# Sorting the first layer's batches by expert too, so that pairs of them share one weight product: a two-layer mixture-of-experts kernel on one NeuronCore

## The chip, the core and the metric

The kernel runs on one NeuronCore of a Trainium2 chip. TensorE (PE) multiplies matrices into PSUM, VectorE (DVE), ScalarE (ACT) and GpSimd (POOL) do the rest, each works through its own instructions in order, and SyncE (SP) issues most DMAs. The metric is the device time of one execution in microseconds. All data are float32.

## The reference, cut to what matters

```
x: (16, 256, 256)   cond: (16, 8)          # 16 batches, 256 rows, width 256; 8 experts
# layer 0: each batch by the expert of its largest cond
e = argmax(cond, -1)
up, gate = x @ W_up[e].T + b_up[e], x @ W_gate[e].T + b_gate[e]        # width 512
x = x + (silu(up) * gate) @ W_down[e].T + b_down[e]
# layer 1: each batch by its two largest experts, weighted, plus one shared expert
w, sel = top_k(softmax(cond), 2); w = w / w.sum()
mlp(x, g, u, d) = (gelu(x @ g) * (x @ u)) @ d                          # width 1024
out = x + sum_k w_k * mlp(x, skill[sel_k]) + mlp(x, shared)
```

## The kernel before

Batches lie transposed (128 partitions, two halves of the width, 256 rows). The product of one 128x128 weight block and one batch's 256 columns is one matmul; the trace records each as two halves. A batch alone needs 24 matmuls in layer 0 and 48 in layer 1.

**Pairs.** Two batches that use the same weights form a 2x2 block product: weight blocks A11 to A22 against B11, B21 (first batch) and B12, B22 (second). `STEPS` writes this product with seven block products in place of eight (Strassen's idea in Winograd's form): sums of weight blocks (`sums_a`, on POOL, into tiles `s` and `ds`), sums of activations (`sums_b`, on DVE), and results combined from three PSUM banks X, Q and Y (two buffers each; the down product uses A, B and Y). A pair's work on one quarter of the hidden width is a "quarter": seven steps of two matmuls, copies by ACT, combinations by DVE.

**Layer 0** (class `First`) takes the batches in their own order, each alone: `up(0)`, `up(1)`, and the `down()` of the batch before. Its expert comes from `first_largest` on the logits `lg`. The result goes to `x1d` (a DRAM tensor that layer 1 reads) and to `out_dram`, in rows fixed when the kernel is built (L348, L349, on POOL's queue).

**Layer 1** works on units: eight shared pairs of batches (2i, 2i+1), and 32 (batch, expert) entries sorted by expert with pairs first, of which 24 always form 12 pairs (`NP2`) and 8 are left as singles. The sort (`choices`, `order_of_work`) compares all 32 entries with all 32 on DVE, 1024 elements a step, and is dealt out among layer 0's batches. Expert and batch numbers of the sorted units are read into registers at run time (`held`). Two shared pairs come first, then skill pairs, seven singles, and six shared pairs with the eighth single (`lone`) among the first of them. Each unit adds its result to `out_dram` by an accumulating DMA (`add_out`, L442). The last pair reads what `out_dram` holds into `z` and stores the sum itself (L545, SP's queue).

**The order of the work** is written out by hand. `quarters` lists all quarters; `Line.quarter` at the start of each issues the weight load five quarters ahead (`Q_AHEAD`), POOL's sums and the x load three ahead (`S_AHEAD`), and the x sums one ahead. `Line.main` runs a step and advances a clock; `Line.later` puts work (a quarter's seventh step, its activation, a pair's seven down steps) some ticks behind.

Of the kernel before, what the change touches and what calls it, by code (L numbers as in the profile page):

```python
# [7 lines left out]
F32 = mybir.dt.float32  # L8
# [8 lines left out]
P = 128  # L17
KD = D // P
K0 = H0 // P
KP = H1 // P // 2  # L20
NPR = B // 2
NA = 2 * B

NP2 = (NA - E) // 2
N2 = 2 * S
W0 = KD * H0
WH = W0 // 2
OG = W0 + 2 * K0 + KD
F0 = OG + W0
# [28 lines left out]
def kernel(  # L58
# [4 lines left out]
    w0: bass.AP,  # L63
    w0d: bass.AP,
    wq: bass.AP,
    wd: bass.AP,
# [17 lines left out]
    def square(name):  # L84
        return work.tile([P, NA, NA], F32, tag="bt", name=name, bufs=7)

# [4 lines left out]

    def x_load(pr):
        t = work.tile([P, KD, N2], F32, tag="x0", name=f"x_{pr}", bufs=3)
        nc.sync.dma_start(t, x[pr])
        return t

    xs = {0: x_load(0)}
# [13 lines left out]
    num = const.tile([P, NA], F32, name="num")  # L111

# [4 lines left out]
    idx1 = const.tile([P, B], I32, name="idx1")  # L117
# [17 lines left out]
    at0 = const.tile([1, 1], F32, name="at0")  # L135
    idx0 = const.tile([1, 1], I32, name="idx0")
    first_largest(lg0, 0, at0)
    as_index(idx0, at0, E, E - 1)
    at1 = ats[:, :B]
    m1 = first_largest(lg, 1, at1)  # L140
    as_index(idx1, at1, E, E - 1)
    for i in range(NA):
        nc.gpsimd.memset(num[:, i : i + 1], float(i))


    exs_i = const.tile([P, NA], I32, name="exs_i")
    bs_i = const.tile([P, NA], I32, name="bs_i")
    wsort = const.tile([P, NA], F32, name="wsort")
    nwsort = const.tile([P, NA], F32, name="nwsort")

    def choices():

        hot = [const.tile([P, B, E], F32, name=f"hot_{k}") for k in range(2)]
        nc.vector.tensor_tensor(hot[0], em8b, over_experts(at1), ALU.is_equal)
        lg2 = const.tile([P, B, E], F32, name="lg2")
        nc.vector.tensor_scalar(lg2, hot[0], -2.0, 1.0, ALU.mult, ALU.add)
        nc.vector.scalar_tensor_tensor(lg2, lg2, FLT_MAX, lg, ALU.mult, ALU.min)
        at2 = ats[:, B:]
        first_largest(lg2, 2, at2)
        nc.vector.tensor_tensor(hot[1], em8b, over_experts(at2), ALU.is_equal)  # L160
        nc.vector.tensor_scalar(ats, ats, float(-E), -1.0, ALU.max, ALU.min)
        rw = const.tile([P, B, E], F32, name="rw")
        nc.vector.tensor_tensor(rw, lg, over_experts(m1), ALU.subtract)
        nc.scalar.activation(rw, rw, AF.Exp)
        tot = const.tile([P, B], F32, name="tot")
        nc.vector.tensor_reduce(tot, rw, AX.X, ALU.add)
        nc.vector.reciprocal(tot, tot)
        nc.vector.tensor_tensor(rw, rw, over_experts(tot), ALU.mult)
        wts = const.tile([P, 2, B], F32, name="wts")
        for k in range(2):  # L170
            nc.vector.tensor_tensor(hot[k], rw, hot[k], ALU.mult)
            nc.vector.tensor_reduce(wts[:, k, :], hot[k], AX.X, ALU.add)
        den = const.tile([P, B], F32, name="den")
        nc.vector.tensor_tensor(den, wts[:, 0, :], wts[:, 1, :], ALU.add)
        nc.vector.reciprocal(den, den)
        wsc = const.tile([P, 2, B], F32, name="wsc")
        for k in range(2):
            nc.vector.tensor_tensor(wts[:, k, :], wts[:, k, :], den, ALU.mult)
        nc.vector.tensor_scalar(wsc, wts, SCALE, None, ALU.mult)
        nc.vector.scalar_tensor_tensor(wts, wts, 1.0 - SCALE, wsc, ALU.mult, ALU.add)  # L180
        return wts.rearrange("p k b -> p (k b)")

    def rows_of(t):
        return t.unsqueeze(2).to_broadcast([P, NA, NA])

    def cols_of(t):
        return t.unsqueeze(1).to_broadcast([P, NA, NA])

    def small(name):
        return const.tile([P, NA], F32, name=name)  # L190

    def order_of_work(wts):

        tt, red = nc.vector.tensor_tensor, nc.vector.tensor_reduce
        ab = square("ab")
        rank, count, base, left, pos, t = map(small, ("rank", "count", "base", "left", "pos", "t"))
        paired = small("paired")  # L200
        tt(ab, rows_of(ats), cols_of(ats), ALU.is_equal)
        yield
        red(count, ab, AX.X, ALU.add)
        yield
        low = square("low")
        tt(low, rows_of(num), cols_of(num), ALU.is_gt)
        yield
        tt(ab, ab, low, ALU.mult)
        yield
        red(rank, ab, AX.X, ALU.add)  # L210
        yield

        ci = const.tile([P, NA], I32, name="ci")
        nc.vector.tensor_copy(ci, count)
        nc.vector.tensor_single_scalar(ci, ci, -2, ALU.bitwise_and)
        nc.vector.tensor_copy(count, ci)
        tt(paired, rank, count, ALU.is_lt)
        yield
        tt(ab, rows_of(ats), cols_of(ats), ALU.is_gt)
        yield  # L220
        tt(ab, ab, cols_of(paired), ALU.mult)
        yield
        red(base, ab, AX.X, ALU.add)
        yield
        tt(base, base, rank, ALU.add)

        nc.vector.tensor_scalar(left, paired, -1.0, 1.0, ALU.mult, ALU.add)
        tt(low, low, cols_of(left), ALU.mult)
        yield
        red(t, low, AX.X, ALU.add)  # L230
        yield
        n_paired = const.tile([P, 1], F32, name="n_paired")
        red(n_paired, paired, AX.X, ALU.add)
        yield
        nc.vector.tensor_scalar(t, t, n_paired, None, ALU.add)
        tt(base, base, t, ALU.subtract)
        tt(base, base, paired, ALU.mult)
        yield
        tt(pos, base, t, ALU.add)
        at = square("at")  # L240
        tt(at, rows_of(num), cols_of(pos), ALU.is_equal)
        yield

        def sorted_(dst, v):
            got = square("got")
            tt(got, at, v, ALU.mult)
            red(dst, got, AX.X, ALU.add)

        sorted_(t, cols_of(ats))
        yield  # L250
        as_index(exs_i, t, E, E - 1)
        nb = num[:, :B].unsqueeze(1).unsqueeze(1).to_broadcast([P, NA, 2, B])
        got = square("got")
        tt(got.rearrange("p s (k b) -> p s k b", k=2), at.rearrange("p s (k b) -> p s k b", k=2), nb, ALU.mult)
        yield
        red(t, got, AX.X, ALU.add)
        yield
        as_index(bs_i, t, 0, B - 1)
        sorted_(wsort, cols_of(wts))
        yield  # L260
        nc.vector.tensor_scalar(nwsort, wsort, -1.0, None, ALU.mult)
# [11 lines left out]
    def l0_load(b):  # L273
        e = held(idx1, b, E - 1) if b else held(idx0, 0, E - 1)
        src = w0[bass.ds(e, 1)].rearrange("e p f -> (e p) f")
        w = wp.tile([P, OG], F32, tag="q", name=f"w0u_{b}", bufs=6), wp.tile(
            [P, W0], F32, tag="s", name=f"w0g_{b}", bufs=5
        )
        if b == 0:
            for lo, hi in ((0, WH), (WH, OG)):  # L280
                nc.sync.dma_start(w[0][:, lo:hi], src[:, lo:hi])
                nc.sync.dma_start(w[1][:, lo : lo + WH], src[:, OG + lo : OG + lo + WH])
        else:
            nc.sync.dma_start(w[0], src[:, :OG])
            nc.sync.dma_start(w[1], src[:, OG:])
        wdn = wp.tile([P, W0], F32, tag="ds" if b % 2 else "d", name=f"w0d_{b}")
        nc.sync.dma_start(wdn, w0d[bass.ds(e, 1)].rearrange("e p f -> (e p) f"))
        return w, wdn

    class First:  # L290


        def __init__(self, b):
            self.b = b
            self.w, self.wdn = l0_load(b)
            self.hid = work.tile([P, K0, S], F32, tag="bt", name=f"hid_{b}", bufs=7)

        def up(self, hh):
            b, w = self.b, self.w
            pr, cols = b // 2, bass.ts(b % 2, S)  # L300
            bu = w[0][:, W0 : W0 + K0]
            bg = w[0][:, W0 + K0 : W0 + 2 * K0]
            pu = bank("X", f"pu_{b}_{hh}").rearrange("p (j s) -> p j s", j=2)
            pg = bank("Q", f"pg_{b}_{hh}").rearrange("p (j s) -> p j s", j=2)
            for dst, wt in ((pu, w[0]), (pg, w[1])):
                wt = wt[:, bass.ts(hh, WH)].rearrange("p (c h) -> p c h", c=KD)
                for j in range(2):
                    for c in range(KD):
                        nc.tensor.matmul(  # L309
# [519 lines left out]
```

## Time and profile before

| | |
|---|---|
| median of 3 runs | 1072.04 us (1071.8 to 1072.36) |
| the profiled execution: time, span | 1072.31 us, 1070.7 us |
| busy: PE, DVE, ACT, POOL | 1065.7, 647.8, 310.9, 449.4 us |
| granted TensorE clock | 1.0 |
| TensorE records | 4906, of them 10 of the warm-up spin (6.99 us) |
| DMA | 152.56 MB, 142 GB/s over the span; 306 to 426 GB/s from 8 to 29 us, where layer 0 loads ahead |

In the profile a line such as `L462 DVE TENSOR_TENSOR c<-u,Q 128x512` names the line of the kernel, the engine, the operation and the tiles; a duration is that of one instruction or of a merged group (`x8`); a bracket tells how long the engine was idle before it and what it waited for. A matmul record lasts 380 ns but a new one starts every 216 ns, so TensorE's pace is read from starts. The span is the time from the first to the last instruction; the execution's own time is 1.6 us longer.

### The profile page before, as it was taken

How to read it: one execution, taken by the hardware profiler on the slowest of the kernel's cores; microseconds unless marked ns; L12 is line 12 of the kernel's file. 1: busy time of each engine (PE TensorE's matmuls, PEld its weight loads, DVE VectorE, ACT ScalarE, POOL GpSimd, SP SyncE). 2: the span in 40 equal slices, each digit the busy share in tenths (PEclk: the TensorE clock that was granted, in tenths of full speed). 3: DMA queues.
4: the chain of work that ended last, by engine and by line, in shares of the span. 5: the costliest groups of instructions: out<-in, count | busy, mean ns of one | idle time of the engine just before them, and what ended most of it. 6: DMA issues, size and time to landing. Idle time of an engine off the chain costs nothing.

```text
span 1070.7 us, 13745 instructions
## 1 busy us (share of the span) xinstructions
PE 1065.7 (100%) x4906; PEld 932.0 (87%) x4906; DVE 647.8 (61%) x985; ACT 310.9 (29%) x507; POOL 449.4 (42%) x514
## 2 busy tenths in 40 slices
PE   9999999999999999999999999999999999999998
PEld 7888888888888888888888888888888888888887
DVE  5842234877778877877777876311112467777774
ACT  2111114333333333333333333111111333333331
POOL 0111145656635754665466542010002745664520
PEclk9999999999999999999999999999999999999999
DMA  8656763633553354345425532556656443454132
GB/s 331 214 194 222 267 232 104 212 106 90 138 138 99 98 138 132 91 113 138 115 90 131 138 96 77 163 138 202 180 168 203 142 152 106 126 138 107 51 80 39
DMA packets 50805, 152.56 MB, mean 142 GB/s; under 512 B 5298, under 2 KB 16178, under 8 KB 47154
## 3 DMA queue, kind: packets, MB, share of 16 engines
q1 hardware_dynamic: 36690, 131.24, 36.3%
q0 software_dynamic: 14048, 20.45, 10.7%
q8 instruction: 39, 0.64, 0.2%
q14 instruction: 28, 0.23, 0.1%
HBM read 130.70 MB, written 20.97 MB: 142 GB/s over the span
## 4 chain that ended last, share of the span: by engine, by line
PE 100%; DVE 0%; issue 0%
PE X L475 19%; PE Y L475 13%; PE Q L475 13%; PE dX L517 10%; PE dQ L517 6%; PE dY L517 6%; PE pg L309 5%; PE pg L590 5%; PE po L608 5%; PE po L337 5%; PE pu L309 5%; PE pu L590 5%; PE spin L105 1%; DVE idle L102 0%; DVE ys L541 0%
## 5 line engine op out<-in xcount | busy, mean ns | idle before, releaser
L458 ACT ACTIVATE u<-X 128x512 f32<-128x512 f32 x240 | 143.2, 597 | 408.1 <-PE X L475 407.8
L442 POOL DMA_DIRECT2D out_dram<-ys x46 | 47.8, 1040 | 380.0 <-ACT ys L618 138.2
L475 PE MATMUL X<-xt,s 128*128 128x256 f32 x640 | 164.8, 380 | 0.1
L475 PE MATMUL Y<-xt,q 128*128 128x256 f32 x640 | 164.3, 379 | 0.0
L475 PE MATMUL Q<-xt,s 128*128 128x256 f32 x640 | 164.2, 379 | 0.0
L501 DVE TENSOR_TENSOR bt<-c 128x1024 f32<-128x1024 f32 x80 | 106.9, 1336 | 83.8 <-ACT c L499 83.8
L475 PEld LDWEIGHTS X<-xt,s 128*128 128x128 f32 x640 | 120.9, 190 | 18.7 <-issue 2.3
L475 PEld LDWEIGHTS Y<-xt,q 128*128 128x128 f32 x640 | 121.5, 190 | 17.0 <-DVE c L462 0.4
L475 PEld LDWEIGHTS Q<-xt,s 128*128 128x128 f32 x640 | 121.6, 190 | 16.5
L462 DVE TENSOR_TENSOR c<-u,Q 128x512 f32<-128x512 f32 x160 | 108.8, 680 | 27.7 <-ACT u L458 25.4
L462 DVE TENSOR_TENSOR c<-u,Y 128x512 f32<-128x512 f32 x160 | 108.5, 678 | 9.3 <-PE Y L475 9.3
L419 POOL TENSOR_TENSOR s<-q 128x256 f32<-128x256 f32 x80 | 68.9, 862 | 81.7 <-PE Q L475 62.0
L600 DVE TENSOR_TENSOR act<-gel,pu 128x512 f32<-128x512 f32 x32 | 22.0, 688 | 124.7 <-PE pu L590 124.7
L499 ACT ACTIVATE c<-c 128x1024 f32<-128x1024 f32 x80 | 84.1, 1052 | 11.3 <-DVE c L462 11.1
L475 PE MATMUL X<-xt,q 128*128 128x256 f32 x320 | 82.1, 379 | 0.0
L517 PE MATMUL dX<-bt,ds 128*128 128x256 f32 x320 | 75.6, 379 | 0.0
L517 PE MATMUL dY<-bt,d 128*128 128x256 f32 x320 | 75.6, 379 | 0.0
L517 PE MATMUL dQ<-bt,ds 128*128 128x256 f32 x320 | 75.6, 379 | 0.0
L421 POOL TENSOR_TENSOR s<-q 128x256 f32<-128x256 f32 x80 | 73.5, 919 | 0.0
L348 POOL DMA_DIRECT2D x1d<-x x16 | 11.1, 696 | 138.3 <-DVE x L345 129.3
L412 DVE TENSOR_TENSOR bt<-bt 128x512 f32<-128x512 f32 x80 | 69.1, 864 | 0.0
L422 POOL TENSOR_TENSOR s<-s,q 128x256 f32<-128x256 f32 x80 | 68.3, 853 | 0.0
(108 smaller groups left out, 1530.9 us busy)
## 6 DMA issues: line engine op xcount, KB each, us to landing
q<-wq_dram SPq DMA_DIRECT2D x112, 512.0 KB, 3.5
d<-wd_dram SPq DMA_DIRECT2D x28, 1024.0 KB, 6.6
xt<-x1d SPq DMA_DIRECT2D x48, 256.0 KB, 4.4
out_dram<-ys POOLq DMA_DIRECT2D x46, 256.0 KB, 6.0
w0d<-w0d_dram SPq DMA_DIRECT2D x16, 512.0 KB, 8.8
w0u<-w_dram SPq DMA_DIRECT2D x15, 517.0 KB, 7.2
w0g<-w_dram SPq DMA_DIRECT2D x15, 512.0 KB, 8.2
x<-x_dram SPq DMA_DIRECT2D x8, 512.0 KB, 3.4
```

The source lines that it names most:

```text
L309: nc.tensor.matmul(dst[:, j, :], lhsT=wt[:, c, bass.ts(j, P)], rhs=xs[pr][:, c, cols], start=(c == 0), stop=(c == KD - 1),)
L412: tt(t[:, 4:6, :], t[:, 0:3:2, :], t[:, 2:4, :], ALU.subtract)
L419: tt(s("S1"), a("A21"), a("A22"), ALU.add)
L421: tt(s("nS3"), a("A21"), a("A11"), ALU.subtract)
L422: tt(s("nS4"), s("S2"), a("A12"), ALU.subtract)
L458: nc.scalar.activation(t, self.banks["X", j], AF.Copy)
L462: nc.vector.tensor_tensor(self.c[j][:, block].rearrange("p m s -> p (m s)"), self.copies[n, j], self.banks[tag, j], op,)
L475: nc.tensor.matmul(self.banks[tag, j][:, bass.ts(m, S)], lhsT=self.q[j][:, m, A_AT[a], :] if a in A_AT else self.s[j][:, m, S_AT[a], :], r ...
L499: nc.scalar.activation(c[:, :, 0, :], c[:, :, 0, :], AF.Gelu_apprx_tanh)
L501: nc.vector.tensor_tensor(t[:, 0:4, :], c[:, :, 0, :], c[:, :, 1, :], ALU.mult)
L517: nc.tensor.matmul(d, lhsT=src[:, j, :], rhs=self.acts[j][:, B_AT[b], :], start=OPENS[k] and j == 0, stop=j == KP - 1, skip_group_check=True,)
L590: nc.tensor.matmul(dst[:, bass.ts(half, S)], lhsT=self.q[j][:, m, 2 * half + c, :], rhs=self.xt[:, c, :], start=(c == 0), stop=(c == KD - 1),)
```

## The change

Layer 0 becomes units like layer 1's. Batch 0 (`First`) is still computed alone and at once. The 15 batches behind it are sorted by expert, with pairs first; whatever the data, four pairs (`NP1`) can be formed, and seven batches stay single.

- `order_of_work(n, at, layer)` is the sort for both layers, rewritten: one key (the entry's expert times n plus its number, plus 4096 if it has no partner) and its rank. For layer 0 it runs on 16x16 comparisons, all at once, at the start (batch 0 gets key 0 and sorts to an unused place); for layer 1 it is dealt out by `next(routing)`: six steps between batch 0's two quarters, five at each of the next two quarters, one at each after that.
- Layer 0's weights are laid out as layer 1's (`wq0`, `wd0`), with the bias columns behind the blocks. A pair of layer 0 is two quarters of seven steps and seven down steps of two matmuls, three ticks apart, begun 18 ticks after its last quarter. `act` adds the biases (`scalar_tensor_tensor`, Silu); `early` adds the residual and the down bias.
- A layer 0 single is cut in pieces (`ups`: both quarters, 16 matmuls; `downs`: 8), one piece after each quarter of a layer 0 pair or of the first shared pairs (`among`). One single's quarters run before the first pair.
- Batch numbers of layer 0 and of the shared pairs (which now pair batches as sorted, `batches_at`) are read at run time, for loads and for the writes of `x1d` and `out_dram`. Three shared pairs (`NF`) stand ahead of the skill pairs.
- Results are sent at the start of the next quarter, behind POOL's sums there (`done`, `send`), but at once for the second last unit. The last pair's stores go to SP's queue for one batch and to ScalarE's for the other.

```diff
-    for b in range(B):
-        firsts.append(First(b))
...
-        if b < B - 2:
-            firsts[b].up(0)
-            firsts[b].up(1)
-            if b:
-                firsts[b - 1].down()
...
+    l0_first = First(next(names), 0, B - 1)
+    l0_pairs = [Pair(next(names), 0, 2 * i) for i in range(NP1)]
+    l0_ones = [Single(next(names), 0, 2 * NP1 + i) for i in range(NS1)]
+    shared = [Pair(next(names), 1, None, (2 * i, 2 * i + 1)) for i in range(NPR)]
...
+    units = [*l0_pairs, *shared[:NF], *pairs, *ones[:-1], *shared[NF:]]
...
+    pieces = [p for u in l0_ones[1:] for p in (u.ups, u.downs)]
+    pieces.insert(0, l0_ones[0].downs)
+    places = [a for u in units[: NP1 + NF] for a in among[u]]
...
+    for j in range(l0_first.kp):
+        l0_first.load_q(j, 2)
+    l0_first.load_d()
+    m1 = first_largest(lg, 1, at1)
...
+    for _ in order_of_work(B, sort1, 0):
+        pass
+    routing = choices()
+    for j in range(2):
+        l0_ones[0].load_q(j)
+    l0_ones[0].load_x()
+    l0_pairs[0].load_q(0)
+    line.at = 0
+    l0_first.up(0)
+    line.ahead(0)
+    for _ in range(6):
+        next(routing)
+    line.at = 1
+    l0_first.up(1)
+    line.ahead(1)
+    l0_first.downs()
+    l0_ones[0].ups()
...
+                if self.layer:
+                    nc.gpsimd.dma_start(row(out), ys[:, :, t, :], accum_op=ALU.add)
+                else:
+                    nc.gpsimd.dma_start(row(x1d), ys[:, :, t, :])
+                    nc.gpsimd.dma_start(row(out), ys[:, :, t, :])
...
+                    queue = (nc.sync, nc.scalar)[t]
+                    store = queue.dma_start(self.out[t][:, c, :], dst)
```

## The prediction

> **What bounds the kernel now.** I read the page first, for which engine is full, then the chain of waits and the timeline of the places that the change touches.
>
> ```profile
> PE 1065.7 (100%) x4906; PEld 932.0 (87%) x4906; DVE 647.8 (61%) x985; ACT 310.9 (29%) x507; POOL 449.4 (42%) x514
> ...
> PE 100%; DVE 0%; issue 0%
> ```
>
> TensorE is never idle between its first matmul and its last, so the time is the number of matmuls times their pace, plus the two ends. The chain of waits in order of time (start and length in us, engine, line, records) gives the pace:
>
> ```profile
> 8.59 1.73 PE pu L309 x8
> ...
> 22.40 3.45 PE po L337 x16
> ...
> 32.76 3.45 PE po L337 x16
> ```
>
> One batch of layer 0 (24 matmuls, which the trace records as 48 halves) repeats every 32.76 - 22.40 = 10.36 us: 0.216 us a half, 0.432 us a matmul, 0.863 us a pair's step of two. A change gains by removing matmuls; it loses wherever another engine makes TensorE wait, which so far none does.
>
> **Matmuls.** Removed: 15 batches x 24 = 360 in layer 0. Added: four pairs x 42 (two quarters of 14, and 14 down) and seven singles x 24 = 336. Layer 1 keeps its own. 24 fewer is exactly one batch's row: **-10.36 us**. The built instruction order of the two kernels has the same difference (2429 matmuls against 2453), so "it does not do what it says" is no rival. Biases, residuals and the copies of the bias columns lie on other engines and cost TensorE nothing while those keep up; the rest of the sum asks where they don't.
>
> **The start.** So far expert numbers for batch 1 were ready at 6.5 us and loads ran ahead. Now nothing behind batch 0 can be loaded before 15 batches are sorted, and VectorE, which sorts, also makes batch 0's activations. From the timeline (start, length, engine, line):
>
> ```profile
> 5.03 0.29 DVE L126 TENSOR_REDUCE m<-lg 128x16 f32<-128x128 f32 x1 [2.06 <-DMA lg<-cond_dram]
> 5.35 0.29 DVE L128 TENSOR_TENSOR cand<-lg,m 128x128 f32<-128x128 f32 x1
> ...
> 22.89 1.22 DVE L201 TENSOR_TENSOR ab<-ats 128x1024 f32<-128x1024 f32 x1
> 24.14 1.22 DVE L203 TENSOR_REDUCE count<-ab 128x32 f32<-128x1024 f32 x1
> ...
> 31.36 0.18 DVE L215 TENSOR_SCALAR ci<-ci 128x32 int32<-128x32 int32 x1
> 31.57 0.18 DVE L216 CAST count<-ci 128x32 f32<-128x32 int32 x1
> ```
>
> Steps of 128 elements follow each other every 0.32 us, small ones every 0.21, those of 1024 every 1.25; 256 elements (16x16) interpolate to 0.45. From 5.03: four steps of the choice 1.3, three more 0.7, ten of 256 4.5, eight small 1.7, the index 0.2: experts at 13.4 us; two more of 256 and an index: batches at 14.5. Two activations of batch 0 (0.44 each, the pitch of L324) end at 15.4, when TensorE, from 8.59, has done batch 0's two quarters (15.5). Then the order puts ten steps of the second choice (the kind of L154 to L166, 2.9 us by their pitch) ahead of the second quarter's activations: those run 18.3 to 19.2. TensorE has used up the first quarter's by 17.2, so it waits and ends batch 0 at about 20.7 instead of 18.95: **+1.7** (0.9 if the logits land 0.8 us sooner, 256 KB less of x ahead of them at the 331 GB/s of that slice; 2.5 if 0.8 later).
>
> *Loads behind it.* The earlier kernel took 0.7 us from the index (2.97) to the first weight load (3.69), so the second batch's quarters are issued at 14.1 and 14.7, its x at 15.3. A 512 KB load lands in 3.5 us in layer 1, a 256 KB one in 4.4, but w0g took 8.2 in layer 0 with loads piled up. SP has nothing to issue from about 6.5 to 14, so the queue is empty and I take layer 1's: x at 19.7, before TensorE is free, cost nothing. With 8.2 it lands at 23.5: +2.8.
>
> *The clock.* In the spin, a weight load takes 0.34 us until 6.03 and 0.19 after 6.7: the array starts slow and speeds up after about 5 us of work. [...] The sum goes by the row: no gap there, no fall, nothing added.
>
> *The squares.* The sort for layer 1 (32x32) is dealt out one step to a quarter, but three go between the second batch's two activations. VectorE: first activations to 25.2 (matmuls end 24.15), x sums 1.6, six small steps 1.25, three squares 3.7, second activations 0.9: 32.7. TensorE needs the Y bank that they read at 20.7 + 16 x 0.432 + 5 x 0.863 = 31.9. So +0.9 alone, and more with contention:
>
> ```profile
> 307.32 0.43 DVE L413 TENSOR_TENSOR bt<-bt 128x256 f32<-128x256 f32 x1
> ...
> 315.73 1.93 DVE L413 TENSOR_TENSOR bt<-bt 128x256 f32<-128x256 f32 x1
> 316.15 1.21 POOL L419 TENSOR_TENSOR s<-q 128x256 f32<-128x256 f32 x1
> ```
>
> The same VectorE step takes 0.43 us alone and 1.93 beside GpSimd's sums, which now run here too. I take **+1.4** (0.9 to 2.6, the upper end being three squares and the x sums at the slowed means).
>
> **Layer 0's pairs with singles.** One pair and one single are 66 matmuls, 28.5 us. VectorE in that time: 8 combinations 5.4, bias and product 2.7, sums 3.1 to 4.7, x sums 1.6, residuals and results 3.6, single 2.7, four squares 4.9: 24 to 26 us, and some 2.5 of waits for ScalarE (1.05 per quarter in L501's row). Nearly full. Where a single's down product follows dY, its Y bank is read only some 0.2 us before it is needed; slowed steps make that a wait of 0.4, twice: **+0.8** (0 to 3).
>
> *POOL.* Row numbers are now read at run time, so each write to x1d or out waits for the write before it to land; before, they went to fixed rows and did not. What such a wait looks like in the timeline of POOL:
>
> ```profile
> 343.25 1.08 POOL L442 DMA_DIRECT2D out_dram<-ys  x1 [4.65 <-DVE ys L543]
> 350.84 1.07 POOL L442 DMA_DIRECT2D out_dram<-ys  x1 [6.51 <-DVE c L462]
> ```
>
> and, from the page's list of DMA issues (count, size, us from issue to landing):
>
> ```profile
> x1d<-x POOLq DMA_DIRECT2D x16, 256.0 KB, 5.1
> out_dram<-x POOLq DMA_DIRECT2D x16, 256.0 KB, 5.5
> ```
>
> From issue to the next issue 7.6 us, of which 7.0 is that one's landing. A pair with the single behind it writes three rows of each: two such waits and four issues, 2 x (5.5 + 0.6) + 1.7 = 14 us, up to 19 at 8.5 a wait. Behind it on POOL stand the next sums: two quarters and half a down, 3.4 us each. 24 us, up to 29, of 28.5. They are asked for three quarters ahead, so at the median they are done 2 to 9 us early. The tightest is the block sent in the last quarter of the first shared pair, which must also wait for the next pair's x1d loads (about 6 us): 2 us early. Cost zero; if that cover goes, up to 5. The first four writes of x1d, in the window of 8 to 60 us, landed in a median of 2.6 us. [...]
>
> **The end.** The last stores now go to rows read at run time and wait for the second last pair's accumulating writes, which also wait for each other.
>
> ```profile
> 1054.46 1.08 POOL L442 DMA_DIRECT2D out_dram<-ys  x1 [25.49 <-DVE ys L541]
> 1056.88 1.06 POOL L442 DMA_DIRECT2D out_dram<-ys  x1 [1.32 <-DVE ys L541]
> 1059.24 9.02 SPq L545 DMA_DIRECT2D out_dram<-ys  x4
> 1067.48 0.42 DVE L541 TENSOR_TENSOR ys<-dz,dQ 128x256 f32<-128x256 f32 x1 [1.30 <-PE dQ L517]
> ```
>
> These two landed in 4.5 and 4.3 us. In a row: 1054.5 + 5.1, then 4.5: 1064.1. The last two of the four stores need results of about 1066.2 and 1067.9 anyway. Zero; at the row's slowest landing (9.0 each) +7. ScalarE's queue takes two of the stores; no row shows it, and I take SP's 0.34 and 1.7.
>
> **Sum**, on the profiled execution (1072.31 us, span 1070.7): -10.36 + 1.7 + 1.4 + 0.8 = -6.5, so 1065.8. The median lies 0.27 under that execution: **1065.5 us**. The terms' own ends (0.9 + 0.9 + 0, and 2.5 + 2.6 + 3) give 1063.5 to 1069.8.
>
> **Rivals.**
> - *All waits hidden* (1061.7 to 1063.4): what speaks for it is that VectorE was 61% busy and nothing ever stopped TensorE; against it, the order above puts ten steps and then three squares in front of activations that TensorE needs. 12%.
> - *The loads come late*: x at 23.5 as in layer 0's rows, +2.8, with the forecast's terms at or above their middle: 1068.3 to 1069.9. For: TensorE has one batch of cover. Against: an empty queue. 18%.
> - *POOL's chain of writes becomes the bound* (slower). At 8.5 us a wait (three pairs of L442's run-time rows stand 7.6, 8.55 and 9.1 us apart) the block is 19, with 3 of waiting for x1d loads and sums at 3.4 the cycle is 32 to 33 us against TensorE's 28.5; over four pairs 4 x 4.5 = 18, less some 5 of lead: +13, so 1072.0 - 10.4 + 3.1 + 13 = 1078. It decides from 28.5 us a cycle, a wait of about 8 us; plain writes show 5.1 and 5.5, 7.9 at most. 12%.
> - *That chain by half*, eating the gain (1069.9 to 1074.2): 5%.
>
> **Numbers.** The forecast's own case has 53%. A measurement here can tell about 0.2% (2.1 us) from no change. Faster by more: 53 + 12 + 18 = 83%; within: 5%; slower: 12%. The range leaves out the last two rivals (17%) and the lower end of the first (3%): 1062.2 to 1070.0.
>
> **What would show it.** Right: 4858 TensorE records; one gap of 1 to 2.5 us near 17 us before the second half of batch 0's down product, released by VectorE, one near 32 us at a pair's sixth step, none over 0.6 after 60 us. Wrong: gaps before L407's matmuls released by POOL's sums (the slower rival), gaps at 20 us released by a DMA (loads), a last store more than 3 us after the last matmul (the end), or no gap at all.

## The result, and the profile after

The changed kernel takes 1067.12 us (median of 6 runs, 1065.57 to 1067.8) against 1072.03 for the kernel before (6 runs, 1071.8 to 1072.36): ratio 0.9951, 95% interval 0.9938 to 0.9964. That is 4.9 us less. The profiled execution is one of the quicker ones: 1065.70 us, span 1064.1. The six times fall in two groups, 1065.57 and 1065.7 with a granted clock of 0.999 and 1.0, and 1067.07 to 1067.8 with 0.998; what parts them is taken up with the experiments.

The page of the changed kernel, its line of busy times, and its chain of waits by engine:

```profile
PE 1055.8 (99%) x4858; PEld 921.7 (87%) x4858; DVE 681.1 (64%) x1070; ACT 323.6 (30%) x516; POOL 472.7 (44%) x570
...
PE 97%; DVE 1%; DMA 1%; issue 0%; SPq 0%; ACT 0%; DVEq 0%
```

TensorE has 48 records and 9.9 us less, and is no longer on the whole chain. What it waited for (us in total, times, longest):

```profile
PE Y L407 <- DVE act L565: 2.4, 1, 2.4
...
PE po L575 <- DVE act L565: 0.7, 1, 0.7
```

Two gaps, both released by VectorE's activations, at the two places that the prediction named. The timeline of TensorE there (start, length, line, idle time before):

```profile
14.71 1.89 PE L575 MATMUL po<-act,d 128*128 128x256 f32 x8
17.33 1.99 PE L575 MATMUL po<-act,d 128*128 128x256 f32 x8 [0.73 <-DVE act L565]
...
26.07 1.03 PE L407 MATMUL X<-x,q 128*128 128x256 f32 x4
...
29.70 1.10 PE L407 MATMUL X<-x,s 128*128 128x256 f32 x4
33.19 1.13 PE L407 MATMUL Y<-x,q 128*128 128x256 f32 x4 [2.38 <-DVE act L565]
```

From one step of a pair to the next should be 0.863 us; from 29.70 to 33.19 it is 3.49, so the second gap costs 2.63. VectorE in the same stretch:

```profile
16.80 0.86 DVE L565 SCALAR_TENSOR_TENSOR act<-pl,q,gel 128x256 f32<-128x256 f32 x2
...
28.22 1.22 DVE L158 TENSOR_TENSOR sq_ys<-num 128x1024 f32<-128x1024 f32 x1
29.35 1.75 DVE L159 TENSOR_TENSOR sq_z<-ats 128x1024 f32<-128x1024 f32 x1
31.13 1.22 DVE L160 TENSOR_REDUCE count<-sq_z 128x32 f32<-128x1024 f32 x1
32.27 0.86 DVE L565 SCALAR_TENSOR_TENSOR act<-pl,q,gel 128x256 f32<-128x256 f32 x2
```

The second gap ends when both activations have ended (33.13), the first with the first of its two. Behind 60 us no slip is over 0.35 us (the two longest, 0.3 each, at 171 and 680 us).

The profiled execution, term by term (starts from TensorE's timeline; the end is the time less the start of the last down step: 1065.55 before, 1058.70 now):

| term | predicted | measured | how |
|---|---|---|---|
| matmuls | -10.36 | -10.36 | 48 records x 0.216 |
| start | +1.7 | +0.4 | first pair starts at 26.07; 40 matmuls behind before's 8.42 are 25.70 |
| squares | +1.4 | +2.6 | 3.49 - 0.86 |
| rest of layer 0 | +0.8 | +0.5 | what is left of 1058.70 - 1065.55 = -6.85: small slips, some of them in layer 1 |
| end | 0 | +0.2 | 7.00 against 6.76 |
| sum | -6.5 | -6.6 | 1065.70 - 1072.31 |
| clock | 0 | 0 here, about +1.6 in four of six runs | the two groups of times |

### The profile page after: what moved, and what is told of

Its sections match the earlier page's. It is cut to its first block, busy times and chain, and to the rows that moved or that the text cites. A ratio compares the mean times of both kernels' runs of the same rounds, so it can differ in the third digit from the quotient of the medians.

```text
span 1064.1 us, 14030 instructions
## 1 busy us (share of the span) xinstructions
PE 1055.8 (99%) x4858; PEld 921.7 (87%) x4858; DVE 681.1 (64%) x1070; ACT 323.6 (30%) x516; POOL 472.7 (44%) x570
## 4 chain that ended last, share of the span: by engine, by line
PE 97%; DVE 1%; DMA 1%; issue 0%; SPq 0%; ACT 0%; DVEq 0%
PE X L407 21%; PE Y L407 14%; PE Q L407 14%; PE dX L458 11%; PE po L575 7%; PE p L546 7%; PE pl L546 7%; PE dQ L458 7%; PE dY L458 7%; DMA x<-x_dram 1%; PE spin L96 1%; DVE sq_z L159 0%; SPq L235 0%; ACT L433 0%; SPq L284 0%
## 5 line engine op out<-in xcount | busy, mean ns | idle before, releaser
L407 PE MATMUL Y<-x,q 128*128 128x256 f32 x704 | 181.5, 380 | 2.4 <-DVE act L565 2.4
L407 PE MATMUL Q<-x,s 128*128 128x256 f32 x704 | 180.7, 379 | 0.0
L407 PE MATMUL X<-x,s 128*128 128x256 f32 x672 | 173.0, 380 | 0.0
L407 PEld LDWEIGHTS Y<-x,q 128*128 128x128 f32 x704 | 132.8, 190 | 22.8 <-DVE act L565 2.8
L407 PEld LDWEIGHTS Q<-x,s 128*128 128x128 f32 x704 | 133.8, 190 | 18.2
L407 PEld LDWEIGHTS X<-x,s 128*128 128x128 f32 x672 | 127.1, 190 | 19.1 <-issue 2.1
L575 PE MATMUL po<-act,d 128*128 128x256 f32 x384 | 89.8, 380 | 0.8 <-DVE act L565 0.7
L407 PE MATMUL X<-x,q 128*128 128x256 f32 x352 | 90.3, 379 | 0.0
L546 PE MATMUL pl<-x,q 128*128 128x256 f32 x368 | 86.9, 379 | 0.0
L546 PE MATMUL p<-x,q 128*128 128x256 f32 x368 | 86.9, 379 | 0.0
L575 PEld LDWEIGHTS po<-act,d 128*128 128x128 f32 x384 | 72.8, 190 | 11.4 <-DVE act L565 1.1
```

The lines of the kernel that those rows point to most:

```text
L407: nc.tensor.matmul(self.banks[tag, j][:, bass.ts(m, S)], lhsT=self.q[j][:, m, A_AT[a], :] if a in A_AT else self.s[j][:, m, S_AT[a], :], r ...
L546: nc.tensor.matmul(dst[:, bass.ts(half, S)], lhsT=self.q[j][:, m, 2 * half + c, :], rhs=self.xt[:, c, :], start=(c == 0), stop=(c == KD - 1),)
L575: nc.tensor.matmul(self.po[:, bass.ts(c, S)], lhsT=self.d[:, 2 * c + half, j, :], rhs=self.acts[j][:, bass.ts(half, S)], start=(j == 0 and ...
```

## The experiments

**The squares.** The three steps of layer 1's sort go behind the second batch's activations, one to a quarter.

```diff
-            for _ in range(5 if self.at < 4 else 1):
+            for _ in range({2: 5, 3: 2}.get(self.at, 1)):
```

> The three 1024-element steps of layer 1's sort (one of them at L158, L159 and L160 each) are taken from ahead of the second batch's second activations; two small steps stay there and the squares follow one to a quarter. Nothing else is changed. Theory: the 2.4 us gap of TensorE at Y L407 exists because the second activations stand behind these squares in VectorE's order, so it goes whole: the wait of Y L407 on L565 is under 0.3 us, and the profiled execution falls by 2.3 to 2.6 us, to 1063.1 to 1063.4. Rival A, the squares only move: VectorE is nearly full in the first pair's quarters too, so the same 1.1 to 1.8 us steps each end some wait there, and less than half of it (0 to 1.2 us) is won. Rival B, the activations are late for ScalarE's or POOL's sake and the gap stays at 2 us or more. On the spread of the times (1065.57 to 1067.8 with granted clocks 1.0 to 0.998): if it is the gap that makes the granted clock fall in some executions, then without it all runs of this kernel lie within 0.6 us and the clock is 1.0 in each; if the spread comes from elsewhere (the warm-up), it stays about 2 us.

Measured: 1062.96 us (5 runs, 1062.56 to 1063.57; ratio to before 0.9917, 0.9903 to 0.993), clock 1.0 in four runs and 0.999 in one. TensorE's waits for data in its profile come down to a single one, of 0.2 us. The gap goes whole, so rivals A and B fall: the squares find room a quarter later, VectorE being busy for 89.27 of the 112 us from 60 to 172. The median falls by 4.2, more than the gap's 2.6; the other 1.6 is the second group of times, which is gone too. The gap at the first `po` is gone as well, though nothing was moved there: this execution's TensorE left the warm-up 0.98 us later (8.78 against 7.80) and the first pair still starts at 26.16. It starts 0.1 later than in the changed kernel, as VectorE's activations end 0.1 later (17.76 against 17.66): VectorE sets that moment, not TensorE.

**More squares.** The opposite, on the changed kernel:

```diff
-            for _ in range(5 if self.at < 4 else 1):
+            for _ in range({2: 5, 3: 8}.get(self.at, 1)):
```

> The opposite of the first: three more steps of the routing (two of them of 1024 elements, some 1.2 us each, and one of three small operations) are put ahead of the second batch's second activations. Theory: the gap at Y L407 grows by what they take, 2.5 to 3.2 us, to 4.9 to 5.6 us, and the time by the same, to 1068.2 to 1068.9 in an execution that keeps its clock. On the clock: if a gap of this length makes the granted clock fall, some 3.4 us of the records after it run at half rate and cost up to another 2 us in most runs (1070 to 1071, granted clock 0.998 or less); if the clock does not mind gaps, the spread is the same 2 us as with the shorter gap.

Measured: 1070.92 us (11 runs, 1070.69 to 1072.79), clock 0.996 or 0.997 in every run. The gap is 6.3 us, longer than expected: L161 took 1.74 beside POOL. The granted clock fell, as the second half of the expectation has it. Busy time by stretch of this kernel (window, its length, busy time and count of PE, PEld, DVE, ACT and POOL, granted clock, DMA):

```profile
34.00:34.50 0.50, 0.00 (x0) 0.00 (x0) 0.47 (x2) 0.00 (x0) 0.44 (x1) 0.89 0.00 0
34.50:41.00 6.50, 3.85 (x9) 3.13 (x10) 4.84 (x12) 0.00 (x0) 0.00 (x0) 0.50 0.27 89
```

A mean of 0.89 over half a microsecond puts the fall at 34.4; half rate (0.50) lasts until about 41.2 (the next microsecond has a mean of 0.89): 6.8 us, where the expectation has 3.4. TensorE resumed at 37.15, so about 4 us ran at half rate and 2 were lost.

**The choices.** The ten steps go behind batch 0's second activations.

```diff
-    for _ in range(6):
-        next(routing)
     line.at = 1
     l0_first.up(1)
     line.ahead(1)
+    for _ in range(6):
+        next(routing)
```

> The ten steps of the routing of layer 1 (L205 to L213) that stood between batch 0's two activations on VectorE go behind the second one; the squares stay. Theory: TensorE's wait of 0.7 us (0.9 us of lost time) at the first po is the pitch of these ten steps, so it goes and the time falls by 0.7 to 0.9 us, to 1064.8 to 1065.0 profiled; the gap at Y L407 stays at 2.4 us or grows a little, since the ten steps are still ahead of it. Rival: the work saved here is only moved, since VectorE does the same steps ahead of the second batch's activations, and the 2.4 us gap grows by what the first one loses: no change, 1065.4 to 1066.

Measured: 1067.12 us (5 runs, 1065.55 to 1068.08), no change. The first gap is gone in the profile; the second is 2.8 us. That is the rival's outcome: the second gap grew by 0.4 while the first went. There was little to win in this execution, since TensorE started 0.74 later (8.54 against 7.80): the first pair starts at 25.90 here and at 26.07 in the changed kernel. VectorE ends the second gap 0.2 later (33.36 against 33.13). This profiled execution (1067.29 us) belongs to the slower group, so it can show what parts the groups. Its stretches, with the same columns:

```profile
33.50:34.00 0.50, 0.50 (x3) 0.45 (x4) 0.50 (x1) 0.00 (x0) 0.00 (x0) 1.00 0.00 0
34.00:34.50 0.50, 0.50 (x3) 0.41 (x2) 0.50 (x2) 0.00 (x0) 0.00 (x0) 0.56 0.42 58
34.50:37.00 2.50, 2.50 (x7) 1.93 (x7) 1.78 (x3) 0.00 (x0) 0.00 (x0) 0.50 0.78 262
37.00:37.50 0.50, 0.50 (x3) 0.41 (x2) 0.00 (x0) 0.00 (x0) 0.00 (x0) 0.52 1.07 345
```

TensorE is back at work at 33.41, and the clock falls 0.65 us later, at about 34.1, to come back at 37.5: 3.4 us at half rate, 1.7 lost. In the changed kernel's profile the same gap was 2.4 us and the clock stayed at 1.0 (1.00 in each stretch from 32 to 40 us). All traces stand side by side behind the filled gap.

**Both moves together.**

> Both moves together, the ten steps and the three squares. If both terms of the sum are priced rightly and independent, the two gaps go together and the profiled time falls by 3.0 to 3.5 us, to 1062.2 to 1062.7, which is the count of matmuls alone (1072.31 - 10.36 = 1061.95) and 0.3 to 0.7 for the small slips that stay in layer 0. If the steps only move their wait, it is 1064 or more.

Measured: 1063.03 us (5 runs, 1062.82 to 1063.59), as with the squares alone. The first pair starts at 25.75, 0.4 earlier; in the profiled execution a weight load of layer 1 that landed in 8.0 us at 861 us gave 0.9 back. Nothing is won beyond the squares that these runs can tell.

**One square less**, for the clock (`{2: 5, 3: 4}` in the line of the first experiment).

> The changed kernel with one of the three squares (L160) less ahead of the second batch's second activations; the other two stay. Between the kernel without squares there (no gap, all clocks 1.0 or 0.999, 1062.96 us) and the changed kernel (gap 2.4 to 2.8 us, 1065.57 to 1067.8). If a gap costs its length and only a gap near 2.8 us costs the clock as well, the gap is now 1.1 to 1.3 us, every run keeps its clock, the times lie within 1 us of each other, and the median is 1064.0 to 1064.4. If every gap puts the clock in danger, some runs show 0.998 and the median is 1065 or more.

Measured: 1064.6 us (6 runs). Five lie between 1063.78 and 1064.91 with clock 1.0; the gap is 1.1. The sixth is 1068.43 with 0.998; it has no trace, and what it lost is open.

**The gap filled.** The changed kernel, with matmuls that nobody reads:

```diff
+                    if k == 5 and j == 0 and self is l0_pairs[0]:
+                        fill = bank("B", "fill")
+                        for _ in range(6):
+                            nc.tensor.matmul(
+                                fill[:, :S], lhsT=self.q[j][:, 0, 0, :], rhs=self.x["B11"],
+                                start=True, stop=True,
+                            )
                     line.main(UP, lambda j=j, k=k: self.up(j, k))
```

> The changed kernel as it was (three squares ahead of the second batch's second activations, gap of 2.4 to 2.8 us), with six more matmuls of 256 columns, 6 x 0.432 = 2.6 us, put in front of the waiting sixth step of the first pair; they write a free bank that nobody reads. The wait itself is not shortened, but TensorE works through nearly all of it. If it is the idleness that takes the clock, every run keeps 1.0 (or 0.999), all lie within 1 us, and the median is 1065.4 to 1066.2, as the changed kernel's best runs are: 1.2 us under its median of 1067.12. If the clock falls for another reason, or does not explain the two groups of times, the median stays at 1067 and the spread at 2 us.

Measured: 1065.8 us (5 runs, 1065.64 to 1066.85), clock 1.0 in all five. TensorE's timeline:

```profile
30.68 2.75 PE L525 MATMUL fill<-x,q 128*128 128x256 f32 x12
33.47 1.13 PE L407 MATMUL Y<-x,q 128*128 128x256 f32 x4
```

The sixth step starts at 33.47, 0.3 later than without these matmuls, but no run loses the clock (1.0 in five of five), where four of six did (0.998). These runs differ from the changed kernel's in TensorE's idle time and not in the wait for VectorE, and the clock loss is gone; this accounts for the 1.3 us between this median and that of the changed kernel.

**Which idleness.** The longest waits in the traces, one execution of each kernel, and the granted clock there (a time is that of TensorE's resuming; 1.0 without a stretch is the mean of the execution; the last three rows are the runs with more pairs and the fifth the one with doubled writes, all told below):

| run | TensorE waited | granted clock |
|---|---|---|
| changed kernel | 2.38 us, to 33.19 | 1.00 from 32 to 40 |
| one square less | 1.09 us, to 32.27 | 1.0 |
| choices later | 2.77 us, to 33.41 | 0.50 from about 34.1 to 37.5 |
| more squares | 6.32 us, to 37.15 | 0.50 from about 34.4 to 41.2 |
| writes twice | 11.35 us, to 211.82 | mean 0.56 from 205 to 211, 0.51 from 211 to 216, 1.00 from 216 to 222 |
| six pairs | 2.5 us, the longest of nine | mean 0.98 from 100 to 200 |
| five pairs | 2.50 us, to 191.39 | 1.00 from 190 to 191, mean 0.57 from 191 to 195, 1.00 from 195 to 196 |
| five pairs, single moved | 1.68 us, to 147.03 | 1.0 |

A wait of 2.38 us went with a clock of 1.00, one of 2.50 with a fall. What decides between them is not shown: the waits of executions without a trace are unknown, those of the changed kernel's four slower runs among them, and no run moved a wait and left its length. A fall does fit the two groups of times: 3.4 us at 0.50, as with the choices later, are 1.7 us lost of a span of 1066, a mean of 0.998 (an estimate from that trace), and the slower four show 0.998 and 1.6 us more.

**POOL's writes.** On the kernel with the squares later, to see when the slower rival would have come true:

```diff
+                    for _ in range(2):
                         nc.gpsimd.dma_start(row(x1d), ys[:, :, t, :])
                         nc.gpsimd.dma_start(row(out), ys[:, :, t, :])
```

> On the kernel with the squares later (1062.96 us): each of layer 0's writes to x1d and to out is issued twice, with the same data. A pair with its single then has a block of 12 writes instead of 6 on POOL: 7.4 to 11.6 us as measured, so 16 to 23 us now, which is the 19 us of the slower rival, and with 13.6 us of sums a cycle of 30 to 37 us against TensorE's 28.5. Reading 1, from the trace: POOL's sums are done 13 to 26 us before TensorE uses them (not 2 to 9), so the lead absorbs four cycles of 1.5 to 8 us each except at the end: 0 to 5 us slower than 1062.96, waits of L407 or L458 on POOL at most in the last cycle. Reading 2, the prediction's cover of 2 to 9 us: 8 to 15 us slower, with waits on POOL in every cycle from the second pair on.

Measured: 1079.98 us (5 runs; ratio to before 1.0071, 1.0058 to 1.0084), 17.0 more than without the second writes. TensorE's waits (lines lie one lower here) and the last of POOL's blocks:

```profile
PE X L408 <- POOL s L356: 13.6, 2, 11.3
```

```profile
186.98 0.68 POOL L332 DMA_DIRECT2D x1d<-ys  x1
...
210.24 0.73 POOL L355 TENSOR_TENSOR s<-q 128x256 f32<-128x256 f32 x1
```

The block is 23.3 us, POOL's cycle 34.3 (blocks start at 118.30, 152.69 and 186.98). Four cycles of 5.8 us too many are 23, less a lead of 11.4: 12, against 13.6 waited, in two places (2.3 at 149 us, 11.3 at 212). A half-rate stretch at the second (mean granted clock 0.56 from 205 to 211 and 0.51 from 211 to 216), 4.1 us of it with TensorE at work, adds about 2, and a wait of 1.6 for VectorE at 243 us the rest. Neither reading came out whole: the waits stand in two places and not in every cycle, nearer to reading 1, and the loss is above the range of reading 2. The rival's mechanism is real; its price was not paid because the block is short.

**More pairs**, on the same kernel (`NP1 = 6`, then `NP1 = 5`; right only for data that hold so many).

> On the kernel with the squares later: six pairs and three singles instead of four and seven (right for this input alone, whose batches hold seven pairs). 12 matmuls fewer by count, 24 records x 0.216 = 5.18 us: 1057.8 us if all else stays hidden. Rival A: from the fourth pair on pairs stand back to back (18.1 us each on TensorE) and VectorE, with some 18 to 20 us of work for a pair and one 1.2 us square in each quarter, becomes the bound: waits of Y or X L407 on VectorE's L394 or L441, 1 to 4 us in all, 1059 to 1062. Rival B: POOL, with 10.2 us of sums and four writes (7 to 10 us) a pair, becomes the bound: waits on s or ds, some 1 to 5 us.

> As with six pairs, but five pairs and five singles, so that nearly every pair still has a single among its quarters. 6 matmuls fewer, 12 records x 0.216 = 2.59 us: 1060.4 us. If a pair's price is its matmuls alone, this and the one with six pairs lie on one line through 1062.96 (2.59 us a pair); if singles among the quarters are what hides VectorE's work, this one gains its 2.59 us and the next pair less.

Measured: six pairs 1071.76 us (11 runs, 1070.21 to 1073.75), five pairs 1066.06 (5 runs, 1065.77 to 1067.14), against 1062.96 with four. Fewer matmuls, and slower by 8.8 and 3.1: the one line falls, and with six pairs rival A holds at a higher price. With six, waits on VectorE add up to 9.3 us from 113 us on, and VectorE is busy 93.85 of the 100 us from 100 to 200. With five pairs TensorE waits in one place, the seam between the first two shared pairs, and the clock falls there too (mean 0.57 from 191 to 195). TensorE's timeline there, and then VectorE's:

```profile
187.76 1.13 PE L407 MATMUL Y<-x,q 128*128 128x256 f32 x4 [0.89 <-DVE c L394]
191.39 2.05 PE L407 MATMUL Q<-x,s 128*128 128x256 f32 x4 [2.50 <-DVE c L394]
```

```profile
182.31 1.37 DVE L349 TENSOR_TENSOR bt<-bt 128x256 f32<-128x256 f32 x1
183.61 1.75 DVE L347 TENSOR_TENSOR x<-x 128x512 f32<-128x512 f32 x1
...
187.03 0.68 DVE L394 TENSOR_TENSOR c<-u,Y 128x512 f32<-128x512 f32 x1
```

The next pair's x sums stand between two pairs in VectorE's order; with a single's 16 matmuls at the seam (four pairs) they have 7 us, here they hold up the next pair's first combination.

**The single moved** to that seam (`del places[7:13]`), away from the one between the fourth and fifth pair:

> Five pairs and five singles with the squares later, as before (1066.06 us, waits of 0.9 and 2.5 us at the second shared pair's first quarter, near 187 us), but the last single is moved from between the fourth and the fifth pair to between the first and second shared pair, where that wait was. If it is a single between two pairs that gives VectorE the time for the next pair's x sums, the waits of L407 on c L394 near 187 us go with their clock loss (-3.4 and about -1.5 us), and waits of 0.7 to 1.6 us on L491 come at the seam that lost its single, as with six pairs: 1061 to 1063. If the wait came from loads or writes of x1d, it stays where it was and the time is 1066 or more.

Measured: 1064.69 us (5 runs, 1063.68 to 1065.56), clock 1.0 throughout. The waits near 187 are gone; at the seam that lost its single and behind it there are new ones, 1.3, 1.7 and 0.5 us at 142, 147 and 175, and 0.5 at 112. The time is 1.7 above what was expected at most, since there were four such waits and not one or two. That a single at a seam is what pays for VectorE's work there is shown.

## Why the prediction was right or wrong

*Matmuls.* Right: 4858 records, 10.36 us, and the rest is what the waits give back.

*The start.* Right in mechanism, mis-sized: 0.4 for 1.7. The ten steps took 2.9 us as worked out. But the batches' numbers were ready at 13.2 and not 14.5: logits landed 0.4 earlier (4.65), and the sort took 8.6 us, not 9.5; activations and steps then overlapped a little, so the second quarter's activations ended at 17.66, not 19.2. The lower end, 0.9, was reasoned from the logits alone and was still too high. The wait itself lost 0.9 us (idle 0.73, where the sign named was 1 to 2.5); 0.6 of that is TensorE's earlier start, 7.80 against 8.42, since in this execution the spin's weight loads take 0.34 us until 4.33 and 0.19 from 5.66 on, and before 0.34 until 6.03 and 0.19 from 6.71 on. No term covered that.

*Squares.* Right in place and cause, mis-sized: 2.6 for 1.4. VectorE was ready about when the term has it, at 33.13 (32.7 without contention, 33.3 with the term's +1.4). Its first activations ended at 23.74 and not at 25.2; then x landed late for it (its sums wait 1.04 us and start at 24.79), the sums were slowed (L348 took 0.83, L349 of the same size 0.42), and L159 took 1.75 for 1.22 beside POOL's sums. But TensorE was there at 30.56 and not at 31.9, because the start had cost less. The gap grew by what the start term had too much: +3.0 measured for both, +3.1 predicted, since VectorE's end sets the end of the second gap, whatever TensorE waited before. That is why the sum for the profiled execution is right to 0.1 us, and not because each term was known; that VectorE's own errors made up for each other is luck.

*The clock.* This step failed. "No gap there, no fall" goes by the row of the kernel before, a clock of 1.0 where TensorE is 100% of the chain. That row has no gap and shows nothing of what one costs the clock, so the zero was the author's estimate, and it was not asked again for the second gap, whose own range reached 2.6. In the profiled execution it held (1.00 behind both gaps, 0.73 and 2.38 us). Four of six runs lose about 1.6, which is the whole difference between 1065.5 predicted and 1067.12. Where a trace has a fall, it cost 1.7 with the choices later (3.4 us at 0.50, TensorE at work throughout) and about 2 with more squares (6.8 us at 0.50, TensorE at work in 4 of them).

*Loads.* Right: x was there in time for the second batch's TensorE work, and no gap at 20 us was released by a DMA. Where x was late, it was late for VectorE.

*Layer 0's pairs and singles.* +0.5 for 0.8, but not as two waits of 0.4: one slip of 0.3 at 171 us (0.2 of it idle), and smaller ones. "Nearly full" was 24 to 26 us of 28.5 (84 to 91%); measured are 78% (86.96 of the 112 us from 60 to 172). Six pairs show what full is.

*POOL.* Zero was right, the cover was not. The block takes 7.5 to 11.6 us, not 14:

```profile
119.70 0.69 POOL L331 DMA_DIRECT2D x1d<-ys  x1 [10.99 <-DMA x<-x1d]
122.85 0.69 POOL L331 DMA_DIRECT2D x1d<-ys  x1 [1.74 <-DVE dz L475]
126.61 0.54 POOL L332 DMA_DIRECT2D out_dram<-x  x1
```

A write behind the other stands 3.2 us apart, not 6 to 7.6; the first bracket ends with the predicted wait for a pair's x1d loads. From the list of DMA issues:

```profile
x1d<-ys POOLq DMA_DIRECT2D x8, 256.0 KB, 2.6
x1d<-x POOLq DMA_DIRECT2D x7, 256.0 KB, 4.0
```

The sum had gone by the 5.1 us of all sixteen writes of the kernel before; the first row has the 2.6 of the first four there, the second lies between. From the second pair on POOL's sums are ready 11 to 27 us ahead, not 2 to 9: those ended at 134.9 are first used at 147.6, those at 187.8 at 199.2. The rival would decide from a block of 28.5 less 13.6 of sums, 14.9 us; with the writes doubled it did.

*The end.* +0.2 for 0. The last accumulating writes were no wait; the span ends 3.5 us after VectorE's last result begins, 3.2 before.

*Rivals.* All waits hidden: not so in this kernel, though moving three steps makes it so (1062.96, inside the 1061.7 to 1063.4 given for it). Loads and POOL: not met.

## What to carry to other kernels

Whoever removes matmuls from a full TensorE should ask which engine's order stands in front of the next one: three steps of an index sort cost 4.2 of the 10.4 us here, and one constant moved them away. A gap of TensorE had two prices here, its length and the granted clock (0.50 for 3.4 us and more); in the traces the second fell due at waits of 2.50 us and longer and not at 2.38, so a term of the sum whose range reaches there, as the 2.6 of the squares did, needs both. And the product with fewer matmuls needs more of VectorE (681.1 us busy against 647.8 before): the fifth and sixth pair cost more than they saved, since singles between pairs are the time in which VectorE catches up.

## What the runs showed of the hardware

The granted clock fell to 0.50 in the traces in which TensorE waited 2.50 us (five pairs), 2.77 (choices later), 6.32 (more squares) and 11.35 (writes twice), and the stretch at 0.50 was about 3.4, 3.4, 6.8 and 10 us long. With the choices later it began 0.65 us after TensorE had resumed. The clock was 1.00 behind a wait of 2.38 us in the changed kernel's trace, and 1.0 over the executions whose longest waits were 1.09 us (one square less) and 1.68 us (five pairs, single moved). The six runs of the changed kernel show 0.999 to 1.0 twice and 0.998 four times, with 1.6 us more, so a single profile of it is not enough to know its time.
